# An MoE layer's last experts: down products by rows, then a spread to the tokens by a product with their weights; four last pairs instead of three; more gather buffers

## The chip, the cores and the metric

The kernel runs on 1 core of one Trainium2 chip. The metric is device time in microseconds (us) of one execution. The engines are named as in the profile: PE is TensorE's matrix product and PEld its weight load, DVE is VectorE, ACT is ScalarE, POOL is GpSimd, SP is SyncE, which here only issues transfers. A name with a q (ACTq, SPq) stands for transfers issued from that engine's queue.

## The reference

One layer for 256 tokens of width 512: cross attention over 4096 context tokens and the tokens themselves, then a state space block, then a mixture of experts. Only the last part is touched:

```python
def _L0_ffn_ref(hidden_states, gate_w, wg, wu, wd, sg, su, sd):
    # 256 tokens, HID 512, 32 experts of inner width 192, the best 6 per token
    scores = jax.nn.sigmoid(x @ gate_w)
    topk_w, topk_i = jax.lax.top_k(scores, TOP_K)
    topk_w = topk_w / (jnp.sum(topk_w, axis=-1, keepdims=True) + 1e-20)
    combine = jnp.sum(jax.nn.one_hot(topk_i, N_EXP, dtype=topk_w.dtype) * topk_w[..., None], axis=1)
    g = jnp.einsum('td,edf->tef', x, wg)
    u = jnp.einsum('td,edf->tef', x, wu)
    act = jax.nn.silu(g) * u
    routed = jnp.einsum('tef,efd,te->td', act, wd, combine)
    shared = jax.nn.silu(hidden_states @ sg) * (hidden_states @ su) @ sd
    return routed + shared
```

Here `x` is the layer norm of the residual, and the result is added to the residual. All is float32.

## The kernel before, in words

Attention and the state space block fill about the first 800 us and are not touched. Then the router ranks the tokens of every expert, sorts the experts so that those with the fewest tokens come last, and scatters the tokens' rows into one table in HBM (`xg`), a block of rows for each expert.

**Rounds.** The 32 experts go in 16 pairs, one pair a round (line 1524 on). Pairs 0 to 8 are wide: each expert has a block of 128 rows (`gate_up`, L1430; `down`, L1460). Pairs 9 to 15 are halves: the two experts of a pair share one block, 64 rows each (`gate_up_halves`, L1383; `down_halves`, L1406), and their products with 64 columns of weights run side by side on TensorE. A round n issues, in program order: gate and up of pair n (`ps_egu`, L218 or L1389); the fetch of pair n+2's token rows (`fetch`, L1354, for most pairs an indirect transfer on POOL); the transposes of pair n+1's rows (`xgTp`, L1370, copied out by DVE); the down product of pair n-1; an expert weight load for a later pair (`load_pair`, on POOL); and the transposes of pair n's hidden rows (`hidTp`, L1402 or L1448, copied out by ACT, L1404 or L1450). DVE makes the hidden rows from ACT's `si` and `ps_egu` (L1393, L1396).

**Two ways from the hidden rows to the tokens.**

- Rows (pairs 0 to 12): the down product gives the expert's rows; ACT copies them from PSUM to `y_sb` (L1414, L1472) and writes them to a table `ye` in HBM (L1415, L1474). Later each token gathers its rows from `ye` by an indirect transfer on POOL (`gather`, L1316, one for each of the 6 choices and each of the 2 token tiles, into `yk`) and DVE adds them, times the token's weight, to the residual `x_sb` (`add`, L1327, L1330). A choice whose expert is not in `ye` reads a row of zeros (`ZROW`).
- Spread (the last three pairs, 13 to 15; `TAIL` is 6 experts): `spread_halves` (L1417) multiplies the hidden rows with a matrix `spread` of 128 rows by 256 tokens that holds each row's weight in its token's column, so that the hidden values stand by tokens; ACT and DVE copy them (L1427, L1428, `hidS`). `down_into` (L1452) then makes the down product for both token tiles, three products of 128x512 each, and sums all three pairs in two PSUM tiles `total`. The matrix `spread` is made in round 3 by `weights_back` (L1494 to L1517): masks on DVE (L1500 to L1514), transposes on TensorE (`spreadT`, L1516).

At the end `finish` (L1567) adds `total` to `x_sb` for each token tile, and `store` (L1570) writes it out.

**What sets the order.** A scheduler places the instructions of each engine; every engine takes its own in order. The PSUM pool for down results has three buffers, of which `total` holds two in the last rounds. The gathers of the first token tile are issued in round 13, after pair 12's rows; those of the second after the first's adds. Their buffers come from three rings: the rings of `y_sb` and `xg_sb` (four buffers each) and a ring of its own, `yp` (three). `tc.issue_after(done[n])` keeps adds behind DVE's last hidden result of round n. Lines that the prediction uses: L1330, L1389, L1402, L1411 and L1412 (down by rows of a half pair), L1415, L1424, L1428, L1457, L1516, L1567.

Of the kernel before, what the change touches and what calls it, by code (L numbers as in the profile page):

```python
# [11 lines left out]
FP = mybir.dt.float32  # L12
# [48 lines left out]
TAIL = 6  # L61
# [12 lines left out]
def perceiver_layer(ctx: ExitStack, tc: tile.TileContext, a: dict, out: bass.AP):  # L74
# [65 lines left out]
    def layer(ctx, bounded):  # L140
# [936 lines left out]
        def rows_of(t):  # L1077

            V.tensor_scalar(m["dst"][:, t], m["iota"][:, 0:NE], float(L), None, ALU.mult)
            V.tensor_tensor(m["dst"][:, t], m["dst"][:, t], m["rank"][:, t], ALU.add)  # L1080
            V.tensor_tensor(own, m["hot"][:, t], m["dst"][:, t].unsqueeze(1).to_broadcast([P, TOPK, NE]), ALU.mult)
            V.tensor_reduce(m["rowf"][:, t, :], own, AX.X, ALU.add)
            V.tensor_copy(row[:, t, :], m["rowf"][:, t, :])

        def result_rows():
# [7 lines left out]
            for t in range(NT):  # L1093
                V.tensor_tensor(own, m["hot"][:, t], dst[:, t].unsqueeze(1).to_broadcast([P, TOPK, NE]), ALU.mult)
                V.tensor_reduce(m["rowf"][:, t, :], own, AX.X, ALU.add)
# [220 lines left out]
        def gather(src, rows, t, *rings):  # L1316

            got = []
            for k in range(TOPK):
                pool, tag = rings[k % len(rings)]  # L1320
# [11 lines left out]
        class Rounds:  # L1332


            def __init__(self, ctx, weights):
# [9 lines left out]
                self.rows, self.xgT, self.hid, self.hidT, self.done = {}, {}, {}, {}, {}  # L1345
# [60 lines left out]
            def down_halves(self, n, to):  # L1406
# [5 lines left out]
                TE.matmul(ps, h[:, 1, :], wd[2], start=False, stop=True)  # L1412
                y = self.e4.tile([P, DM], FP, tag="y", name="y_sb")
# [3 lines left out]
            def spread_halves(self, n, by):  # L1417

                h = self.hid.pop(n)

                whole = [pool.tile([P, 2, L], FP, tag=tag, name=name) for pool, tag, name in
                         ((self.ps_t, "t", "hid_sp"), (self.ps_ye, "ye", "rest_sp"))]
                for i in range(2):
                    TE.matmul(whole[i][:, 0, :], h[self.half(i), 0:P], by[self.half(i)], start=True, stop=True)  # L1424
                TE.matmul(whole[1][:, 1, :], h[:, P:2 * P], by, start=True, stop=True)
                hs = self.hidT[n] = self.e2.tile([P, 3, L], FP, tag="hidS", name="hidS")
                S.copy(hs[:, 0, :], whole[0][:, 0, :])  # L1427
                self.done[n] = V.tensor_copy(hs[:, 1:3, :], whole[1]).ins  # L1428
# [23 lines left out]
            def down_into(self, n, total, first, last, tiles=range(NT)):  # L1452
                wd = self.down_weights(n)
                h = self.hidT[n]
                for t in tiles:
                    for j in range(3):
                        TE.matmul(total[t], h[:, j, t * P:(t + 1) * P], wd[j],  # L1457
                                  start=(first and j == 0), stop=(last and j == 2))

# [16 lines left out]
        with ExitStack() as rctx:  # L1476
            main = Rounds(rctx, weights)
            yp = rctx.enter_context(tc.tile_pool(name="yp", bufs=3))
# [41 lines left out]
            def spread_last(n):  # L1520
                main.spread_halves(n, spread[:, n - LAST, :])

            got, r_y, r_x, r_k = None, (main.e4, "y"), (main.e4, "xg"), (yp, "yk")
# [52 lines left out]
            with arms.Else():  # L1576
# [20 lines left out]
                for t in range(NT):  # L1597
                    add(gather(ye2, row2, t, (main.e4, "xg")), t)
# [55 lines left out]
```

## Time and profile before

| | |
|---|---|
| median of 6 runs | 992.71 us (990.6 to 993.81) |
| profiled execution, device time | 992.73 us |
| its span, first to last instruction | 990.9 us |
| granted TensorE clock, mean | 0.997 |
| rounds of the experts | about 844 to 982 us |
| last weights and rows off the queues | about 953 us |
| first and last gather issued | 959.42 and 974.69 us |
| last add begins | 978.54 us |
| finishes of the two token tiles begin | 979.87 and 982.38 us |

The page of the profile gives each engine's busy time, the span in 40 slices, the transfers, the chain of work that ended last, and the costliest groups of instructions by line. The timeline lists instructions in order of time: start, length, engine, line, operation, tiles as out<-in with their shape, and how many were merged (x). In brackets stands the engine's idle time just before, and what ended it. A float32 product of 128x512 is two records (x2). Ends of products are modelled and overlap the next one, so costs on TensorE are read from start to start. Times of the table are microseconds from the start of the span.

### The profile page before, as it was taken

The page shows a single profiled execution, that of the slowest core. Times are in us where ns is not written, and L with a number is a line of the kernel's source. Part 1 is how long each engine was busy: PE and PEld are TensorE (multiplying, and loading weights), DVE is VectorE, ACT ScalarE, POOL GpSimd, SP SyncE. Part 2 cuts the span into 40 slices and gives each one's busy share as a digit, 9 for nine tenths or more (in the row PEclk, how much of TensorE's full clock was granted, in tenths as well). Part 3 has the DMA queues.
Part 4 walks back from the last instruction along what each step waited for, and adds up shares of the span by engine and source line. Part 5 has one row for each costly group of instructions (what it writes and reads, how often), then busy time and mean ns, then how long its engine had stood idle before and what let it go on. Part 6 is the DMA issues. An engine that isn't in the chain of part 4 may idle for free.

```text
span 990.9 us, 8901 instructions
## 1 busy us (share of the span) xinstructions
PE 968.8 (98%) x2742; PEld 456.3 (46%) x2742; DVE 498.5 (50%) x999; ACT 386.2 (39%) x851; POOL 205.6 (21%) x212
## 2 busy tenths in 40 slices
PE   7999999999999999999999999999999999999996
PEld 3444444444444444444444444444465655555442
DVE  4456554454453544534545544468596756422134
ACT  3645444443443444434434434353262822122210
POOL 4443001101100200200200200000013325454523
PEclk9999999999999999999999999999999999999998
DMA  8734132222313304304204112140055553999963
GB/s 318 234 74 116 56 114 91 51 38 111 85 22 127 85 4 145 86 0 149 69 16 141 41 32 65 63 127 1 0 176 178 209 174 117 331 351 352 390 228 113
DMA packets 131580, 125.91 MB, mean 127 GB/s; under 512 B 80225, under 2 KB 99586, under 8 KB 126274
## 3 DMA queue, kind: packets, MB, share of 16 engines
q1 hardware_dynamic: 119216, 77.96, 26.2%
q0 software_dynamic: 7984, 41.16, 11.4%
q10 hardware_dynamic: 4322, 6.11, 1.7%
q8 instruction: 24, 0.39, 0.2%
q14 instruction: 34, 0.28, 0.1%
HBM read 89.02 MB, written 36.19 MB: 126 GB/s over the span
## 4 chain that ended last, share of the span: by engine, by line
PE 93%; DMA 1%; DVE 1%; ACT 1%; POOL 1%; issue 1%; another core or an unknown queue 1%; SPq 0%; POOLq 0%; DVEq 0%; ACTq 0%
PE scT L567 23%; PE oT L592 23%; PE ps_kv L364 17%; PE ps_egu L218 4%; PE ps_self L218 3%; PE ps_v L218 2%; PE ps_o L790 2%; PE ps_ye L1466 2%; PE ps_xbc L218 1%; PE ps_out L984 1%; PE ps_egu L1389 1%; PE ps_k L218 1%; PE ps_sgu L218 1%; PE total L1457 1%; PE xgTp L1370 1%; PE ps_ye L1469 1%
## 5 line engine op out<-in xcount | busy, mean ns | idle before, releaser
L583 DVE TENSOR_TENSOR lacc<-lacc,prT 128x512 f32<-128x512 f32 x256 | 182.9, 715 | 239.0 <-ACT prT L573 238.3
L573 ACT ACTIVATE prT<-scT,bq,rk 128x512 f32<-128x512 f32 x256 | 198.8, 777 | 254.0 <-PE scT L567 241.8
L567 PE MATMUL scT<-qT,kT 128*128 128x512 f32 x536 | 271.6, 593 | 0.0
L592 PE MATMUL oT<-prT,v 128*128 128x512 f32 x528 | 268.3, 592 | 0.0
L567 PEld LDWEIGHTS scT<-qT,kT 128*128 128x128 f32 x536 | 101.1, 190 | 124.9 <-issue 122.2
L592 PEld LDWEIGHTS oT<-prT,v 128*128 128x128 f32 x528 | 100.2, 190 | 125.8 <-issue 115.8
L196 POOL TENSOR_TENSOR rk<-pv,mhalf 128x4 f32<-128x4 f32 x32 | 32.3, 1011 | 369.3 <-DVE pv L195 369.3
L364 PE MATMUL ps_kv<-wkv,fast 128*128 128x512 f32 x112 | 53.4, 592 | 0.0
L254 ACT ACTIVATE sq<-kraw 128x128 f32<-128x128 f32 x128 | 35.6, 278 | 45.2 <-DVE kraw L382 43.1
L364 PE MATMUL ps_kv<-wkv,ctx 128*128 128x512 f32 x112 | 52.8, 592 | 0.0
L364 PE MATMUL ps_kv<-fast,fast 128*128 128x512 f32 x112 | 52.6, 592 | 0.0
L598 DVE TENSOR_TENSOR oacc<-oT,oacc 128x512 f32<-128x512 f32 x64 | 43.7, 683 | 0.0
L364 PEld LDWEIGHTS ps_kv<-wkv,fast 128*128 128x128 f32 x112 | 21.3, 190 | 26.8 <-issue 26.8
L364 PEld LDWEIGHTS ps_kv<-fast,fast 128*128 128x128 f32 x112 | 21.3, 190 | 26.8 <-issue 21.8
L364 PEld LDWEIGHTS ps_kv<-wkv,ctx 128*128 128x128 f32 x112 | 21.3, 190 | 26.8 <-issue 23.7
L358 POOL TENSOR_TENSOR fast<-ctx 128x512 f32<-128x512 f32 x7 | 9.3, 1331 | 113.1 <-PE ps_kv L364 94.2
L382 DVE TENSOR_TENSOR kraw<-ps_kv,fast 128x256 f32<-128x256 f32 x42 | 17.8, 424 | 28.2 <-PE ps_kv L364 28.2
L1441 DVE TENSOR_TENSOR hid<-si,ps_egu 128x128 f32<-128x128 f32 x18 | 5.2, 288 | 53.1 <-ACT si L1439 42.9
L790 PE MATMUL ps_o<-wo,qT 128*128 128x512 f32 x64 | 28.8, 592 | 0.0
L218 PE MATMUL ps_self<-wq,xT 128*128 128x512 f32 x64 | 28.1, 592 | 0.0
L603 DVE RECIPROCAL lacc<-ps_l 128x512 f32<-128x512 f32 x8 | 26.8, 3348 | 0.1
L364 PE MATMUL ps_kv<-fast,ctx 128*128 128x512 f32 x56 | 26.3, 592 | 0.0
(392 smaller groups left out, 1129.9 us busy)
## 6 DMA issues: line engine op xcount, KB each, us to landing
xg<-xn SPq DMA_DIRECT2D x6, 2560.0 KB
ctx<-in_ctxT_dram SPq DMA_DIRECT2D x7, 1024.0 KB
kd<-tr SPq DMA_DIRECT2D x112, 64.0 KB
kT<-kd SPq DMA_DIRECT2D x28, 256.0 KB
ye<-y_sb ACTq DMA_DIRECT2D x22, 256.0 KB
wq<-in_wq_dram SPq DMA_DIRECT2D x4, 1024.0 KB
wo<-in_wo_dram SPq DMA_DIRECT2D x4, 1024.0 KB
w_in<-in_W_inT_dram SPq DMA_DIRECT2D x4, 1024.0 KB
```

The costliest lines, as they stand in the source:

```text
L196: return G.tensor_tensor(dst, v[:, :n], mhalf[:, :n], ALU.pow)
L218: TE.matmul(ps, lhs(k), rhs_of(k), start=(k == 0), stop=(k == KD - 1))
L254: S.activation(sq[:, h, :], raw[:, h, :], AF.Square, accum_out=ss[:, h:h + 1])
L364: TE.matmul(ps, lhs(k), rhs(k), start=(start and k == 0), stop=(k == 1), skip_group_check=True)
L567: scored.append(TE.matmul(sc, kT[:, g, i * P:(i + 1) * P], qT[:, t, heads4(g), :].rearrange("p h q -> p (h q)"), start=True, stop=True).ins)
L573: S.activation(pr, sc, AF.Exp, bias=shift, scale=SCALE if r is None else r[:, i, g:g + 1])
L583: V.tensor_tensor(la, la, pr, ALU.add)
L592: TE.matmul(outs[g, t], v[:, i, g * HD:(g + 1) * HD], pr, start=(n == 0), stop=last)
L598: V.tensor_tensor(ov, outs.pop((g, t)), ov, ALU.add)
L603: V.reciprocal(rl, ps)
L790: TE.matmul(m["ps_o", t], aT[:, t, h, :], wo[j][:, h % 4, :], start=(h == 0), stop=(h == NH - 1))
L1466: TE.matmul(ps[i], h[:, i, :], wd[i], start=True, stop=False)
```

## The change

1. `TAIL` is 8 instead of 6: the last four pairs (12 to 15) are spread, three before. `spread`, the masks and the row of zeros grow or move with it; `result_rows` and `rows_of` use the first 6 of the now 8 rows of a work tile.
2. For the last pairs the order is turned round. The hidden rows are transposed (`turn_hidden_halves`), the down product is made by rows (`down_rows`, now shared with `down_halves`) and copied to SBUF by ACT (`down_here`). Then one product for each token tile, with `spread` as the stationary operand and these rows as the moving one, sums into `total` (`spread`). In round n the down of pair n-1 and the spread of pair n-2 are issued.
3. The ring `yp` has six buffers instead of three, and the gathers no longer use the ring of `y_sb`. The gathers of both token tiles are issued one round earlier (rounds 12 and 13), without waiting for adds in program order; the row fetch of pair 15 is moved ahead of them. Three adds are kept behind round 14's hidden result, nine behind round 15's.

```diff
-TAIL = 6
+TAIL = 8
...
-            def spread_halves(self, n, by):
...
-                whole = [pool.tile([P, 2, L], FP, tag=tag, name=name) for pool, tag, name in
-                         ((self.ps_t, "t", "hid_sp"), (self.ps_ye, "ye", "rest_sp"))]
-                for i in range(2):
-                    TE.matmul(whole[i][:, 0, :], h[self.half(i), 0:P], by[self.half(i)], start=True, stop=True)
-                TE.matmul(whole[1][:, 1, :], h[:, P:2 * P], by, start=True, stop=True)
-                hs = self.hidT[n] = self.e2.tile([P, 3, L], FP, tag="hidS", name="hidS")
-                S.copy(hs[:, 0, :], whole[0][:, 0, :])
-                self.done[n] = V.tensor_copy(hs[:, 1:3, :], whole[1]).ins
+            def down_here(self, n):
+
+                self.y[n] = self.e4.tile([P, DM], FP, tag="y", name="y_sb")
+                S.copy(self.y[n], self.down_rows(n))
+
+            def spread(self, n, by, total, first, last, tiles=range(NT)):
+
+                for t in tiles:
+                    TE.matmul(total[t], by[:, t * P:(t + 1) * P], self.y[n], start=first, stop=last)
...
-            def down_into(self, n, total, first, last, tiles=range(NT)):
-                wd = self.down_weights(n)
-                h = self.hidT[n]
-                for t in tiles:
-                    for j in range(3):
-                        TE.matmul(total[t], h[:, j, t * P:(t + 1) * P], wd[j],
-                                  start=(first and j == 0), stop=(last and j == 2))
...
-            yp = rctx.enter_context(tc.tile_pool(name="yp", bufs=3))
+            yp = rctx.enter_context(tc.tile_pool(name="yp", bufs=6))
...
             for n in range(NP):
                 wide = 2 * n < WIDE
                 (main.gate_up if wide else main.gate_up_halves)(n)
-                if n == LAST + 1:
-                    add(got, 0)
-                    got = gather(ye, row_y, 1, r_y, r_x, r_y, r_x, r_x, r_k)
-                if FIRST <= n + 2 < NP:
-                    main.fetch(n + 2)
+
+                for f in range(n + 2, n + 4 if n == LAST else n + 3):
+                    if FIRST <= f < NP and f not in fetched:
+                        main.fetch(f)
+                        fetched.add(f)
...
                 elif n > LAST:
-                    if n == LAST + 1:
-                        total = [main.ps_ye.tile([P, DM], FP, tag="ye", name="total") for _ in range(NT)]
-                    if n == NP - 1:
-
-                        main.down_into(n - 1, total, False, False, [0])
-                        with tc.issue_after(main.done[n]):
-                            add(got, 1, range(0, TOPK // 2))
-                        spread_last(n)
-                        with tc.issue_after(main.done[n]):
-                            add(got, 1, range(TOPK // 2, TOPK))
-                        main.down_into(n - 1, total, False, False, [1])
-                    else:
-                        main.down_into(n - 1, total, n - 1 == LAST, False)
+                    main.down_here(n - 1)
+                if n == LAST:
+                    got.append(gather(ye, row_y, 0, r_k * TOPK))
+                elif n == LAST + 1:
+                    total = [main.ps_ye.tile([P, DM], FP, tag="ye", name="total") for _ in range(NT)]
+                    got.append(gather(ye, row_y, 1, r_x * 2 + r_k * 4))
+                if n > LAST + 1:
+                    spread_last(n - 2)
+                if n == NP - 2:
+                    add_behind(n, 0, 3)
+                if n == NP - 1:
+                    add_behind(n, 3, 2 * TOPK)
...
-                if n == LAST:
-                    got = gather(ye, row_y, 0, r_k, r_y, r_k, r_x, r_k, r_y)
-                if n < LAST:
-                    (main.turn_hidden if wide else main.turn_hidden_halves)(n)
-                elif n < NP - 1:
-                    spread_last(n)
-            main.down_into(NP - 1, total, False, True)
+                (main.turn_hidden if wide else main.turn_hidden_halves)(n)
+
+            spread_last(NP - 2, [0])
+            main.down_here(NP - 1)
+            spread_last(NP - 2, [1])
+            spread_last(NP - 1)
```

More of the change, by code (lines that the diff above doesn't have):

```diff
@@ L1080, in rows_of @@
             V.tensor_tensor(m["dst"][:, t], m["dst"][:, t], m["rank"][:, t], ALU.add)
-            V.tensor_tensor(own, m["hot"][:, t], m["dst"][:, t].unsqueeze(1).to_broadcast([P, TOPK, NE]), ALU.mult)
-            V.tensor_reduce(m["rowf"][:, t, :], own, AX.X, ALU.add)
+            V.tensor_tensor(own[:, 0:TOPK], m["hot"][:, t], m["dst"][:, t].unsqueeze(1).to_broadcast([P, TOPK, NE]), ALU.mult)
+            V.tensor_reduce(m["rowf"][:, t, :], own[:, 0:TOPK], AX.X, ALU.add)
             V.tensor_copy(row[:, t, :], m["rowf"][:, t, :])
@@ L1093, in result_rows @@
             for t in range(NT):
-                V.tensor_tensor(own, m["hot"][:, t], dst[:, t].unsqueeze(1).to_broadcast([P, TOPK, NE]), ALU.mult)
-                V.tensor_reduce(m["rowf"][:, t, :], own, AX.X, ALU.add)
+                V.tensor_tensor(own[:, 0:TOPK], m["hot"][:, t], dst[:, t].unsqueeze(1).to_broadcast([P, TOPK, NE]), ALU.mult)
+                V.tensor_reduce(m["rowf"][:, t, :], own[:, 0:TOPK], AX.X, ALU.add)
             V.tensor_scalar(m["m8"][:, :, 0:TOPK], m["rowf"], float(ZROW), None, ALU.min)
@@ L1308, in layer, with gather @@
         actx.close()
-        def gather(src, rows, t, *rings):
+        def gather(src, rows, t, rings):
             got = []
-            for k in range(TOPK):
-                pool, tag = rings[k % len(rings)]
+            for k, (pool, tag) in enumerate(rings):
                 yk = pool.tile([P, DM], FP, tag=tag, name="yk")
@@ L1344, in __init__ @@
                     G.memset(z, 0.0)
-                self.rows, self.xgT, self.hid, self.hidT, self.done = {}, {}, {}, {}, {}
+                self.rows, self.xgT, self.hid, self.hidT, self.y, self.done = {}, {}, {}, {}, {}, {}
             def row0(self, n):
@@ L1404, in turn_hidden_halves, with down_rows @@
                 S.copy(self.hidT[n], tp)
-            def down_halves(self, n, to):
+            def down_rows(self, n):
                 wd = self.down_weights(n)
@@ L1412, in down_halves @@
                 TE.matmul(ps, h[:, 1, :], wd[2], start=False, stop=True)
+                return ps
+            def down_halves(self, n, to):
+                ps = self.down_rows(n)
                 y = self.e4.tile([P, DM], FP, tag="y", name="y_sb")
@@ L1415, in down_halves @@
                 nc.scalar.dma_start(to[self.row0(n):self.row0(n) + P, :], y)
-            def spread_halves(self, n, by):
-                h = self.hid.pop(n)
-                whole = [pool.tile([P, 2, L], FP, tag=tag, name=name) for pool, tag, name in
-                         ((self.ps_t, "t", "hid_sp"), (self.ps_ye, "ye", "rest_sp"))]
-                for i in range(2):
-                    TE.matmul(whole[i][:, 0, :], h[self.half(i), 0:P], by[self.half(i)], start=True, stop=True)
-                TE.matmul(whole[1][:, 1, :], h[:, P:2 * P], by, start=True, stop=True)
-                hs = self.hidT[n] = self.e2.tile([P, 3, L], FP, tag="hidS", name="hidS")
-                S.copy(hs[:, 0, :], whole[0][:, 0, :])
-                self.done[n] = V.tensor_copy(hs[:, 1:3, :], whole[1]).ins
+            def down_here(self, n):
[4 more added lines that the diff above has]
+                    TE.matmul(total[t], by[:, t * P:(t + 1) * P], self.y[n], start=first, stop=last)
             def gate_up(self, n):
@@ L1519, in layer, with spread_last, add_behind @@
             FIRST, LAST = HEAD // 2, NP - TAIL // 2
-            def spread_last(n):
-                main.spread_halves(n, spread[:, n - LAST, :])
-            got, r_y, r_x, r_k = None, (main.e4, "y"), (main.e4, "xg"), (yp, "yk")
+            def spread_last(n, tiles=range(NT)):
+                main.spread(n, spread[:, n - LAST, :], total, n == LAST, n == NP - 1, tiles)
+            fetched = set()
+            got, r_x, r_k = [], [(main.e4, "xg")], [(yp, "yk")]
+            def add_behind(n, k0, k1):
+                with tc.issue_after(main.done[n]):
+                    for k in range(k0, k1):
+                        add(got[k // TOPK], k // TOPK, [k % TOPK])
             for n in range(NP):
@@ L1597, in layer @@
                 for t in range(NT):
-                    add(gather(ye2, row2, t, (main.e4, "xg")), t)
+                    add(gather(ye2, row2, t, [(main.e4, "xg")] * TOPK), t)
                     store(t)
```

## The prediction

> **What bounds the kernel now.** I read the page's busy table and slices first, then its chain of waits, then the stretch that the diff touches (the last three of the 16 rounds) in the timeline, TensorE alone first, then all engines. A round is one pair of experts; its start is the first gate-up product (L1389).
>
> ```profile
> PE 968.8 (98%) x2742; PEld 456.3 (46%) x2742; DVE 498.5 (50%) x999; ACT 386.2 (39%) x851; POOL 205.6 (21%) x212
> PE   7999999999999999999999999999999999999996
> PE 93%; DMA 1%; DVE 1%; ACT 1%; POOL 1%; issue 1%; another core or an unknown queue 1%; SPq 0%; POOLq 0%; DVEq 0%; ACTq 0%
> ```
>
> TensorE is busy in every slice, and 93% of the chain is its own products. So a change pays by what it takes out of TensorE's sequence, as long as nothing else becomes the last to finish. The rounds:
>
> ```profile
> 944.72 2.80 PE L1389 MATMUL ps_egu<-w_in,xgT 128*64 128x384 f32 x16
> 948.03 0.64 PE L1411 MATMUL ps_ye<-oacc,hidT 128*64 128x512 f32 x1
> 950.01 0.38 PE L1402 MATMUL hidTp<-ident,hid 128*128 128x128 f32 x2
> 950.32 0.54 PE L1389 MATMUL ps_egu<-lacc,xgT 128*64 128x384 f32 x1
> 956.96 0.54 PE L1389 MATMUL ps_egu<-w_in,xgT 128*64 128x384 f32 x1
> 966.69 0.54 PE L1389 MATMUL ps_egu<-wkv,xgT 128*64 128x384 f32 x1
> 969.42 1.12 PE L1457 MATMUL total<-w_in,hidS 128*128 128x512 f32 x2
> 971.37 1.12 PE L1457 MATMUL total<-wkv,hidS 128*128 128x512 f32 x2 [0.82 <-DVE hidS L1428]
> 980.46 1.02 PE L1457 MATMUL total<-ctx,hidS 128*128 128x512 f32 x2
> 981.32 1.02 PE L1457 MATMUL total<-v,hidS 128*128 128x512 f32 x2
> ```
>
> Start times differ by what a step costs; the printed lengths overlap. One 128x512 product into `total` is 981.32 - 980.46 = 0.86. Round 12, which goes down by rows, takes 950.32 - 944.72 = 5.60; rounds 13 and 14 take 6.64 and 9.73; from round 15's start to the end of the last product it is 981.32 + 0.86 - 966.69 = 15.49, with a stall on VectorE's `hidS` copy inside. The other side of the end, the gathers and adds:
>
> ```profile
> 956.44 0.33 ACTq L1415 DMA_DIRECT2D ye<-y_sb  x1
> 959.42 0.94 POOL L1322 DMA_INDIRECT yk<-ye,row_y  x1 [15.30 <-DMA ye<-y_sb]
> 974.69 1.13 POOL L1322 DMA_INDIRECT yk<-ye,row_y  x1 [0.30 <-issue]
> 978.54 0.75 DVE L1330 SCALAR_TENSOR_TENSOR x_sb<-yk,lacc,x_sb 128x512 f32<-128x512 f32 x1 [0.67 <-DMA yk<-ye,row_y]
> 979.87 0.69 DVE L1567 TENSOR_TENSOR x_sb<-total,x_sb 128x512 f32<-128x512 f32 x1 [0.58 <-PE total L1457]
> 982.38 0.69 DVE L1567 TENSOR_TENSOR x_sb<-total,x_sb 128x512 f32<-128x512 f32 x1 [1.81 <-PE total L1457]
> ```
>
> The adds end at 979.29, and both finishes (L1567) wait for `total`. So TensorE ends the kernel, but the adds are only 0.58 ahead of the first finish: a shorter TensorE tail must not outrun them.
>
> **TensorE, round by round.** Pieces: gate-up of a half pair 969.42 - 966.69 = 2.73; down by rows 950.01 - 948.03 = 1.98; the two transposes of `hid` 950.32 - 950.01 = 0.31; a spread product has the shape of L1457, 0.86.
> - Round 13 becomes a copy of round 12: 5.60 instead of 6.64, -1.04.
> - Round 14 is round 12 plus two spreads: 5.60 + 1.72 = 7.32 instead of 9.73, -2.41.
> - Round 15 to the end: 2.73 + 1.98 + 2 x 0.86 + 0.31 + 0.86 + 1.98 + 3 x 0.86 = 12.16 instead of 15.49, -3.33. The 18 products into `total` and nine spreads of `hid` are gone; eight spreads, three downs and six transposes have come. The 0.82 stall goes with `hidS`; next late there is ACT, below.
>
> Sum -6.78. On the old time axis round 14 starts at 955.92, round 15 at 963.24, the last product ends at 975.40.
>
> **Earlier work.** `spreadT` has eight transposes instead of six; six take 0.81 in the chain, so +0.27, on the path. On VectorE, in the order of the changed kernel, ten mask writes (0.24 each, from the row of five in 1.20) stand between the first pair's two `hid` results, not five: the second result comes at 850.29 + 2.40 = 852.69 instead of 852.13. But TensorE's order there also moves one more gate-up product (0.66) ahead of the transpose that waits 1.07 now. These cancel to about 0; bounds -0.1 and +0.6. The member products grow from 192 to 256 columns (0.36 each, nine of them, perhaps 0.07 more each); VectorE idles 1.64 there, and without that cover they cost 0.6.
>
> **The new hand-offs.** The last pair now runs transposes, ACT copy, down, ACT copy, spread. `hidT`: the copy can start 0.20 after TensorE moves on (950.01 to 950.21 for `y_sb`), takes 0.38, plus 0.05 to wake TensorE: 0.63, under one spread of 0.86. `y_sb`: 0.20 + 0.58 + 0.05 = 0.83 under the other 0.86. The trace shows no such chain at the end of the kernel; bounds 0 (both covered) and 0.63 + 0.83 = 1.46 (no cover). The margins of 0.23 and 0.03 are thin, so I take +0.2.
>
> **Gathers and adds.** The last row write that the gathers wait for is pair 11's (issued at 950.82, one round earlier), not pair 12's. Write to first gather is 959.42 - 956.44 = 2.98 now, so the first starts at 953.80; fetching pair 15's rows stays ahead of it in POOL's queue as it was. No weight load is queued behind. The twelfth issue is 15.27 after the first, 969.07, its add 3.85 later (974.69 to 978.54), ending 973.67. VectorE: three adds stand after the copy of `xgT` (960.52) and before round 15's `hid`, done by 962.77; `hid` is wanted at 966.45. Nine adds follow from 967.11: 9 x 0.75 = 6.75, to 973.86. With the 0.58 seen between last add and finish: 974.44. `total` of the first token tile ends at 974.54 and its finish starts 0.27 later (979.60 to 979.87), 974.81. So TensorE still ends it, by 0.37. The two stores then start 0.8 apart, not 2.5; if the second queued behind the whole landing of the first (2.04 for a row write in the chain of waits), that would be +1.2; I take 0, for the 16 DMA engines are 0.13 busy after 982.4 (windows view). The extra buffers cost nothing: gathers eight to ten (counted from 0) wait for adds done by 963, and the last for one done by 967.9.
>
> When gathers and adds meet now, a gather's issue takes up to 1.29 on POOL instead of 0.94, so they lose at most 0.35 each; most gathers will run before the adds, so I add nothing. The Trainium skill, "SBUF — State Buffer", section "SBUF: two separate sides", says that VectorE with two SBUF inputs and GpSimd lock each other out of a shared port for whole instructions (the first named case only against a GpSimd operation that reads SBUF). That speaks against the change: by this rule the five gathers that would meet adds could lose a whole add of 0.75 each, 3.75 in all, and less the room of 0.37 the sum would be near -2.9 instead of -6.3.
>
> **Sum.** -6.78 + 0.27 + 0 + 0.2 = -6.3. The profiled execution took 992.73 (span 990.9, 1.83 around it); the median of six runs is 992.71, the same within 0.02. So 986.4.
>
> **Rivals.**
> 1. The adds end it (0.16). Now adds without idle cover stand up to 0.91 apart (971.90 to 972.81). Nine at 0.91: 967.11 + 8.19 + 0.58 = 975.88, 1.1 after 974.81, so 987.5; a gather held longer puts it up to 988.5. For it: 0.37 of room. Against it: the gathers start 5.6 earlier.
> 2. The ACT copies are exposed (0.10): the 1.46 instead of 0.2, 987.7. For it: margins of 0.03. Against it: ACT is busy 0.70 us in the last 15.7.
> 3. The time is given back (0.06). ACT twice stands without a visible cause before `si` at 845 to 852 (4.36 and 1.84, put down to "remote"). ACT now feeds TensorE in each of the last steps; such holds there would cost 6.2, so 992.6, no change. For it: the changed code places such holds anew. Against it: the last rounds show none.
> 4. Slower (0.04): late gathers block `hid`. VectorE takes the three adds before round 15's `hid` in order. If the first gather started with round 15 (963.24, 9.4 late) instead of 953.80, the twelfth add would end at 963.24 + 15.27 + 4.60 = 983.11, the first finish 983.69, the second 984.38 against 975.6: +8.8, 995.2. It decides from a first gather at 961.24: 982.38, the second finish now, less 15.27 + 4.60 + 0.58 + 0.69. Against it: even now they start at 959.42, behind a later write.
>
> The forecast itself has 0.64 (985.4 to 987.4). A measurement here can tell about 0.2%, 2 us, from no change: faster takes forecast and rivals 1 and 2, 0.90; same rival 3, 0.06; slower rival 4, 0.04. The range reaches down by the bound of -0.1, covered hand-offs and the runs' own spread (990.6 to 993.81), to 984.4, and up past rivals 1 and 2, to 989.2; rivals 3 and 4 are left out.
>
> **What would show it.** Round 13 at 5.6, 14 at 7.3, 15 to the last product at 12.2 to 12.5; eight products on the spread line and no `hidS`; the first gather near 954; the last add ending before the first finish, whose idle time ends on TensorE; waits of TensorE on ACT in the tail under 0.3 in sum. The prediction is wrong if the finishes wait for adds or gathers, if TensorE's tail shows an idle over 1 us, or if round 0 grows.

## The result, and the profile after

The changed kernel takes 989.67 us (median of 23 runs, 986.49 to 991.87), the kernel before in the same sessions 992.12 (46 runs, 990.47 to 994.96). The ratio is 0.9972, with a 95% interval of 0.9965 to 0.9978: 2.8 us less, where 6.3 were forecast. The direction was right and the size was not. The profiled run of the changed kernel took 986.24 (span 984.5), a little under the fastest of these 23; set against the one profiled run of before (992.73) it shows 6.5 less, about what was forecast, and 0.96 of that lies ahead of round 12 (943.76 against 944.72). So the first trace alone would have passed for a confirmation. The question is what the typical run has on top of it.

The changed kernel's page, busy line and chain of waits:

```profile
PE 963.0 (98%) x2730; PEld 453.6 (46%) x2730; DVE 497.6 (51%) x1000; ACT 388.0 (39%) x854; POOL 204.9 (21%) x212
...
PE 95%; ACT 1%; DVE 1%; POOL 1%; DMA 1%; issue 1%; another core or an unknown queue 0%; SPq 0%; DVEq 0%; ACTq 0%
```

Its timeline, the last three rounds (start, length, engine, line; the brackets hold idle time and releaser):

```profile
949.36 0.54 PE L1388 MATMUL ps_egu<-lacc,xgT 128*64 128x384 f32 x1
...
953.47 0.94 POOL L1321 DMA_INDIRECT yk<-ye,row_y  x1 [10.30 <-DVE hid L1395]
...
954.96 0.54 PE L1388 MATMUL ps_egu<-w_in,xgT 128*64 128x384 f32 x1
...
962.28 0.54 PE L1388 MATMUL ps_egu<-wkv,xgT 128*64 128x384 f32 x1
...
966.36 0.33 ACT L1390 ACTIVATE si<-ps_egu 128x192 f32<-128x192 f32 x1 [3.55 <-PE ps_ye L1410]
...
967.40 6.43 DVE L1329 SCALAR_TENSOR_TENSOR x_sb<-yk,lacc,x_sb 128x512 f32<-128x512 f32 x9
...
968.42 1.21 POOL L1321 DMA_INDIRECT yk<-ye,row_y  x1 [0.70 <-issue]
...
969.86 0.58 ACT L1423 COPY y_sb<-ps_ye 128x512 f32<-128x512 f32 x1 [3.17 <-issue]
...
970.50 1.12 PE L1428 MATMUL total<-y_sb,xc 128*128 128x512 f32 x2 [1.57 <-issue]
...
973.53 2.82 PE L1428 MATMUL total<-y_sb,xc 128*128 128x512 f32 x6
...
975.60 1.48 DVE L1565 TENSOR_TENSOR x_sb<-total,x_sb 128x512 f32<-128x512 f32 x2 [1.76 <-PE total L1428]
```

Rounds 13 and 14 take 5.60 and 7.32, as forecast. Round 15 to the last product takes 973.53 + 2.82 - 962.28 = 14.07 and not 12.16. Its gate-up ends 2.73 after its start, at 965.01, but its silu (L1390, the `si` from which VectorE makes pair 15's `hid`) starts at 966.36, 1.35 late; a usual silu starts 0.12 after the product. The copy of pair 14's rows at 969.86 is late too, and TensorE stands still for 1.57 before it can spread them. The words "issue" and a stale product as releaser say that the profile knows no cause.

A second profile of the same kernel (e1_again) is more typical; timeline:

```profile
968.59 0.33 ACT L1390 ACTIVATE si<-ps_egu 128x192 f32<-128x192 f32 x1 [3.88 <-remote]
...
969.63 6.43 DVE L1329 SCALAR_TENSOR_TENSOR x_sb<-yk,lacc,x_sb 128x512 f32<-128x512 f32 x9
...
970.65 1.21 POOL L1321 DMA_INDIRECT yk<-ye,row_y  x1 [4.12 <-DVE x_sb L1329]
...
976.09 1.29 DVE L1565 TENSOR_TENSOR x_sb<-total,x_sb 128x512 f32<-128x512 f32 x2
```

Here round 15 starts at 962.31, the silu is 3.55 late, `hid` of pair 15 and the nine adds behind it follow, and the twelfth gather waits 4.12 for the fourth add. TensorE ends at 975.56, 0.8 earlier than in the first profile, yet the span is 987.0, 2.5 longer. So TensorE does not end this execution.

**What ends it.** The chain of waits stops at the second finish in every profile. The view of the closing line goes on, with the sequencers' records (engine and q; count; least, median and largest ns; first and last start). The kernel before:

```profile
L1650 POOLq DRAIN  x3: 40/107/6593, 983.5 to 990.6; - x3
L1650 SPq DRAIN  x3: 7/7/7, 989.4 to 990.3; - x3
```

The changed kernel, second profile:

```profile
L1648 POOLq DRAIN  x3: 40/107/6594, 979.6 to 986.7; - x3
L1648 SPq DRAIN  x3: 7/7/41, 984.0 to 986.4; - x3
```

POOL closes with a drain of 6.59 us. In these two profiles the drain stands behind the landing of the last gather, a step of 1.77 on POOL's queue, a branch, and 3.0 to 3.4 without a record. SP closes after the stores. The span ends 0.82 to 0.92 after the later of the two in all 20 profiles of this study (table below); from the start of the last gather to the end of POOL's drain it is 14.7 to 15.7. In the kernel before POOL's drain ends at 990.08 and SP's last wait at 989.35: **two chains, 0.7 apart** (0.6 in a second profile, e9_before), and the prediction saw only the one that passes through TensorE. In the first profile of the changed kernel SP is the later one, by 0.33; in the second POOL, by 2.1.

### The profile page after: what moved, and what is told of

Its sections match the earlier page's. It is cut to its first block, busy times and chain, and to the rows that moved or that the text cites. A ratio compares the mean times of both kernels' runs of the same rounds, so it can differ in the third digit from the quotient of the medians.

```text
span 984.5 us, 8877 instructions
## 1 busy us (share of the span) xinstructions
PE 963.0 (98%) x2730; PEld 453.6 (46%) x2730; DVE 497.6 (51%) x1000; ACT 388.0 (39%) x854; POOL 204.9 (21%) x212
## 4 chain that ended last, share of the span: by engine, by line
PE 95%; ACT 1%; DVE 1%; POOL 1%; DMA 1%; issue 1%; another core or an unknown queue 0%; SPq 0%; DVEq 0%; ACTq 0%
PE scT L567 23%; PE oT L592 23%; PE ps_kv L364 17%; PE ps_egu L218 4%; PE ps_self L218 3%; PE ps_v L218 2%; PE ps_o L790 2%; PE ps_egu L1388 2%; PE ps_ye L1458 2%; PE ps_k L218 1%; PE ps_xbc L218 1%; PE ps_out L984 1%; PE ps_sgu L218 1%; PE xgTp L1369 1%; PE ps_ye L1461 1%; PE ps_ye L1411 1%
```

## The experiments

The columns: ratio to the kernel before on the same chip with its interval; how late round 15's silu starts (its start less round 15's first product less 2.73; 0.11 to 0.17 is on time); start of the last gather; end of POOL's drain; SP's last wait over; end of the span. The first profile of before and of the changed kernel stand ahead. Two kinds of chip show up: e5 to e8 ran on one where the kernel before takes 990.0 and no signal of TensorE is late anywhere; all others where it takes 992.1 to 992.7 and some are. The silu is one signal of several: copies behind later products can be late too.

| kernel | ratio | silu late | last gather | POOL | SP | span |
|---|---|---|---|---|---|---|
| before | 1 | 0.12 | 974.69 | 990.08 | 989.35 | 990.9 |
| changed | 0.9972 (0.9965-0.9978) | 1.35 | 968.42 | 983.28 | 983.61 | 984.5 |
| e1_again | 0.9972 (0.9962-0.9982) | 3.55 | 970.65 | 986.17 | 984.03 | 987.0 |
| e2_three | 1.0004 (0.9995-1.0012) | 0.12 | 975.23 | 990.89 | 987.30 | 991.7 |
| e3_slack | 0.9973 (0.9961-0.9986) | 5.66 | 973.05 | 988.17 | 987.73 | 989.0 |
| e4_vector | 0.9984 (0.9973-0.9994) | 3.80 | 971.42 | 986.14 | 986.57 | 987.5 |
| e5_seven | 0.9953 (0.9940-0.9966) | 0.16 | 967.51 | 982.71 | 980.68 | 983.6 |
| e6_plain | 0.9929 (0.9914-0.9944) | 0.16 | none | - | 980.88 | 981.8 |
| e7_shift | 1.0103 (1.0088-1.0118) | 0.17 | 981.93 | 996.94 | 996.36 | 997.8 |
| e8_before6 | 1.0005 (0.9996-1.0014) | 0.11 | 972.86 | 987.81 | 987.00 | 988.7 |
| e9_before | 1.0000 (0.9989-1.0011) | 0.12 | 974.25 | 989.13 | 988.57 | 990.0 |
| e10_after | 0.9971 (0.9960-0.9982) | 3.90 | 971.58 | 987.28 | 984.66 | 988.1 |
| e11_seven | 0.9955 (0.9939-0.9971) | 5.04 | 967.37 | 982.47 | 985.71 | 986.6 |
| e12_both | 0.9961 (0.9945-0.9977) | 6.90 | 967.56 | 982.51 | 987.09 | 988.0 |
| s1_shift30 | 0.9978 (0.9968-0.9989) | 3.93 | 971.22 | 986.79 | 984.65 | 987.6 |
| s2_shift60 | 0.9990 (0.9980-1.0001) | 4.50 | 973.35 | 989.04 | 987.28 | 989.9 |
| s3_plain | 0.9925 (0.9908-0.9941) | 0.16 | none | - | 981.22 | 982.1 |
| s4_two | 0.9979 (0.9967-0.9992) | 6.45 | 970.77 | 985.43 | 991.21 | 992.1 |
| p1_paced | 0.9960 (0.9947-0.9973) | 0.16 | 969.96 | 985.18 | 982.86 | 986.0 |
| p2_half | 0.9964 (0.9952-0.9977) | 2.24 | 970.92 | 985.86 | 988.47 | 989.4 |

**e1_again**: no edit.

> The changed kernel once more, as a yardstick and for a second profile of it. Theory A (the missing time is TensorE waiting in the last round for ACT's copies of y_sb and hidT, whose start is held): -2 to -4 us against the kernel before; rounds 13 and 14 again take 5.60 and 7.32, and the stretch from round 15's first product to the last product is 12.16 plus the idle time shown on the lines of the spread and down products; more than 1 us of idle there. Rival B (the missing time is lost before round 13, in the stage around the weights of the mask or in the first rounds, and the 1.57 us of idle in the first profile is an accident): the last round takes 12.2 to 12.6, and round 13 starts less than 0.5 us earlier than in the kernel before.

Measured -2.8 again, with the silu 3.55 late and POOL, not TensorE, at the end. Rounds 13 and 14 again take 5.60 and 7.32. Rival B falls: round 13 starts 0.93 earlier than in before, and the last round takes 13.26. Theory A has its number, but the end is not TensorE's.

**e2_three**: the new order with three pairs.

```diff
-TAIL = 8
+TAIL = 6
```

> Down by rows and spread as in the changed kernel, but three last pairs instead of four. TensorE's rounds by the terms of the prediction: 13 and 14 take 5.60 each, 15 takes 12.16, so TensorE would end 8.5 us before the old end; but the row write that the gathers wait for is pair 12's again, so they start near 959.4 on the old axis and their adds end near 979.3, as before. Theory A: the adds end it, first finish near 979.9 and the second 0.8 behind instead of 2.5, so -1.3 to -2 us against the kernel before whatever ACT does; the holds of ACT in round 15 do not matter. Rival B (loss before round 13): the adds end it too, and the same loss lies on top: 0 to +2 us. If it came out at or below the changed kernel (-3 us or more), the fourth pair would be worth nothing.

Measured no change, outside the range of theory A and inside that of rival B, but for a reason that neither had. This trace is the cleanest test of the sum for TensorE; timeline:

```profile
962.06 0.54 PE L1388 MATMUL ps_egu<-wkv,xgT 128*64 128x384 f32 x1
...
971.48 2.82 PE L1428 MATMUL total<-y_sb,xc 128*128 128x512 f32 x6
...
975.23 1.03 POOL L1321 DMA_INDIRECT yk<-ye,row_y  x1 [0.30 <-issue]
...
980.06 1.29 DVE L1565 TENSOR_TENSOR x_sb<-total,x_sb 128x512 f32<-128x512 f32 x2
```

The closing line of the same run:

```profile
L1648 POOLq DRAIN  x3: 40/107/6593, 984.3 to 991.4; - x3
L1648 SPq DRAIN  x3: 7/7/7, 987.3 to 991.1; - x3
```

Round 15 to the last product is 12.24, forecast 12.16, so the new hand-offs through ACT cost nothing when signals come on time. TensorE ends 8 us earlier than before and the kernel gains nothing: the last gather starts at 975.23 as ever (974.69 before), and POOL closes 3.6 behind SP. **The whole gain of the change hangs on the fourth pair, which lets the gathers start a round earlier.**

**e3_slack**: more of TensorE's work between each copy and its use.

```diff
-                if n > LAST + 1:
-                    spread_last(n - 2)
+                if n == NP - 1:
+                    spread_last(n - 3)
...
-            spread_last(NP - 2, [0])
+            spread_last(NP - 3)
             main.down_here(NP - 1)
-            spread_last(NP - 2, [1])
+            spread_last(NP - 2)
             spread_last(NP - 1)
```

> The changed kernel with the same products, but the spreads put one round later, so that between each ACT copy of the last pair and its use TensorE has two spreads (1.72 us) in place of one (0.86): pair 12 spreads in round 15 ahead of hidT(15), pair 13 behind it, pair 14 behind the last down. Theory A (ACT's copies are late in round 15): 1 to 3 us below the changed kernel, -4 to -6 against the kernel before; round 13 and 14 take 5.60, round 15 to the end about 13.9 to 14.3, sum near 25.1 as the products alone cost. Rival B: equal to the changed kernel within 0.5 us. Rival C (TensorE itself stands still in round 15, whoever copies): equal within 0.5 us, with an idle on TensorE that no copy explains.

Measured the same as the changed kernel: theory A in its plain form (thin margins between copy and use) fails. The silu itself is 5.66 late, and this order of the spreads does not hide that; timeline:

```profile
970.99 0.33 ACT L1390 ACTIVATE si<-ps_egu 128x192 f32<-128x192 f32 x1 [6.73 <-remote]
971.21 0.58 ACT L1423 COPY y_sb<-ps_ye 128x512 f32<-128x512 f32 x1
```

**e4_vector**: two of the copies on VectorE.

```diff
-                S.copy(self.hidT[n], tp)
+                (V.tensor_copy if n == NP - 1 else S.copy)(self.hidT[n], tp)
...
-                S.copy(self.y[n], self.down_rows(n))
+                (V.tensor_copy if n == NP - 2 else S.copy)(self.y[n], self.down_rows(n))
...
-                if n == NP - 1:
-                    add_behind(n, 3, 2 * TOPK)
...
+            add_behind(NP - 1, 3, 2 * TOPK)
             spread_last(NP - 2, [0])
```

> The changed kernel with two of the last copies taken off ACT: y_sb of pair 14 and hidT of pair 15 are copied by VectorE, two and three adds deep in its order. Theory A with ACT's own sequencer as the cause (its instructions come late): 1 to 2 us below the changed kernel. Theory A' (the signal of TensorE's product is what comes late, to whoever waits): VectorE starts its copies as late as ACT did, no gain, within 0.5 us of the changed kernel or up to 0.8 slower, because an add of 0.75 stands ahead of a copy. Rival B: within 0.5 us.

Measured 0.9984, against the changed kernel in the same session (e1_again) 0.8 us slower by the medians, with overlapping intervals. The time fits theory A', but alone it does not clear ACT: the silu, still on ACT, is 3.80 late here too, and VectorE's two copies stand behind the late `hid`. The semaphore records of e3_slack say more: the signals of the gate-up, down and spread products that end at 965.4 to 969.0 are recorded between 970.91 and 971.10, and the silu (970.99) and the copy behind it follow at once. The products run ahead; the news that they are done comes late, in a bunch. So TensorE's signals are late, and not ACT.

**e5_seven**: one gather buffer more, so that the twelfth gather waits for the third add, ahead of pair 15's `hid`, and not for the fourth, behind it.

```diff
-            yp = rctx.enter_context(tc.tile_pool(name="yp", bufs=6))
+            yp = rctx.enter_context(tc.tile_pool(name="yp", bufs=7))
```

> The changed kernel with seven gather buffers in place of six, so that the twelfth gather waits for the third add (before round 15's hid) and no longer for the fourth (behind it). Theory P (the end is set by POOL: from the landing of the last gather to the end of the span it is 12.5 us in every trace so far, 978.45 to 990.91 in the kernel before, 974.16 to 986.99 in the second profile of the changed one; the last gather is late because it waits behind hid(15)): the last gather is issued before 968.5 and lands before 972, POOL's chain ends near 984, and the time falls to -4.5 to -6 us against the kernel before, 2 to 3 below the changed kernel. Rival T (TensorE's tail sets the end, through the finishes and the stores): within 0.5 us of the changed kernel.

Measured -4.7 us: theory P (POOL's chain sets the end) holds, T (TensorE's tail does) falls. POOL still closes 2 us behind SP.

**e6_plain**: gathers replaced by plain transfers.

```diff
-                G.indirect_dma_start(out=yk, out_offset=None, in_=src,
-                                     in_offset=bass.IndirectOffsetOnAxis(ap=rows[:, t, k:k + 1], axis=0))
+                nc.sync.dma_start(yk, src[(t * TOPK + k) * P:(t * TOPK + k + 1) * P, :])
```

> The changed kernel with its twelve gathers replaced by plain transfers of fixed rows of ye on SP's queue: it leaves out which rows are added. Theory G (TensorE's signals reach ACT late in round 15 because POOL issues gathers one behind the other at that time): signals on time, silu of pair 15 starts within 0.2 us of the end of its gate-up product, the tail takes 12.2 to 12.5, -5.5 to -7.5 against the kernel before. Theory F (late signals come with the load of TensorE's own instructions): signals as late as in the changed kernel, 1.5 us or more in round 15; time -4 to -6, since POOL's end is early here too.

Measured -7.0, but this chip shows no late signal in any kernel, so it decides nothing between G (POOL's gathers make the signals late) and F (the loads of TensorE's own instructions do). It does bound the change: with the gathers off POOL, the new tail of TensorE is worth 7.

**e7_shift**: small products at the start.

```diff
+        d = ps_d.tile([P, 8], FP, name="d")
+        for _ in range(48):
+            TE.matmul(d, ident, ident[:, 0:8], start=True, stop=True)
```

> The changed kernel with 48 small products (128x8, never read) ahead of TensorE's first work, where it stands idle until 5.47; they shift by 96 instructions where its instruction loads fall (16 KB each, 256 instructions apart by the records), so the load seen at 962 to 966 should come 8 to 11 us earlier. Theory F: no signal later than 0.7 us in round 15, hid(15) near 966.5, the last gather lands before 972.5, -4.5 to -6.5 against the kernel before if the small products are hidden, and at most 3 us more if not. Theory G: round 15 as late as in the changed kernel, -2 to -3.

Ill made: a 128x8 product of two f32 passes took 0.43, 20.65 in all, and most of it showed (+10.2). It says one thing: with signals on time and six buffers, the twelfth gather starts 14.09 after the first (967.84), not 17 to 17.7 as in e1_again and e10_after.

**e8_before6**: the kernel before with gathers free of its adds.

```diff
-            yp = rctx.enter_context(tc.tile_pool(name="yp", bufs=3))
+            yp = rctx.enter_context(tc.tile_pool(name="yp", bufs=6))
...
-                    got = gather(ye, row_y, 1, r_y, r_x, r_y, r_x, r_x, r_k)
+                    got = gather(ye, row_y, 1, r_x, r_y, r_x, r_y, r_x, r_y)
...
-                got = gather(ye, row_y, 0, r_k, r_y, r_k, r_x, r_k, r_y)
+                got = gather(ye, row_y, 0, r_k)
```

> The kernel before with the buffers alone: six yk buffers and the second token tile in the free xg and y buffers, so that no gather waits for an add. Gathers then come every 1.25 us from 959.42 on, the last issue near 973.2 and not 974.69. Theory P: POOL ended the kernel before by 0.7 us (its last drain ends 990.08, SP's last wait is over at 989.41), so -0.4 to -0.9, and then SP's stores end it. Rival T: 0.0 within 0.2.

Measured no change, against what P was taken to expect. P is not at fault, the premise was: the twelfth gather starts 15.23 after the first, as in before (15.27). Its gathers were not waiting for buffers; beside adds each takes up to 1.36 instead of 0.94. Buffers alone bring nothing.

**e9_before, e10_after, e11_seven, e12_both**: four kernels on one chip; e12 has the edits of e3 and e5.

> The kernel before, unchanged, for a profile on the same chip as the three that follow. By all theories 0.0 within 0.2 us against itself. What it tells: whether TensorE's signals are late here near the first gate-up products of the rounds (2.1 to 2.4 us in every profile of the first chip, none in the four profiles of the second), and which chain ends the kernel: theory P expects POOL's last drain to end 0.5 to 1 us behind SP's last wait, and 12.2 to 12.8 us from the landing of the last gather to the end of the span.

> The changed kernel, unchanged, on the same chip. Theory P with late signals as a matter of the chip: with signals on time, hid(15) is ready near 966.5 on the first chip's axis, the twelfth gather is issued 1.5 us behind it, and the time is -4.3 to -6 against the kernel before; with late signals as on the first chip -2.3 to -3.2. Rival (the changed kernel is always 2 us worse than the same with seven buffers): -2.3 to -3.2 with signals on time too.

> Seven gather buffers, as run before on another chip (-4.7 there). Theory P: -4.3 to -5.5 here too, whether signals are late or not, because its twelfth gather waits for nothing in round 15; with signals on time within 0.5 us of the changed kernel, with late ones 1.5 to 2.5 below it.

> Seven gather buffers, and the spreads one round later as in the run that gave TensorE more work between a copy and its use. Theory P: POOL's chain ends it as with seven buffers, so within 0.4 us of that kernel. Rival T: up to 1.6 us below it where signals are late, for TensorE's waits on ACT go.

Measured 0, -2.9, -4.5 and -3.9. The chip shows late signals. In e11 the gathers are free (last at 967.37) and POOL is done at 982.47, but now SP ends it at 985.71: pair 15's `hid` is late, so are the adds behind it and the finishes. e12's more patient order does not help, for the adds wait for `hid`, not for spreads. Round 9 starts at 926.61 (before) and 926.70 (changed), so in this pair of profiles the earlier stages cost 0.1.

**s1_shift30, s2_shift60**: is it TensorE's own instruction loads? 30 or 60 small bf16 products at the start, hidden in its first idle time (0.96 and 1.76 us long).

```diff
+        zb = zp.tile([P, P], mybir.dt.bfloat16, name="zb")
+        G.memset(zb, 0.0)
+        d = ps_d.tile([P, 8], FP, name="d")
+        for _ in range(30):
+            TE.matmul(d, zb, zb[:, 0:8], start=True, stop=True)
```

> The changed kernel with 30 small bf16 products (128x8, never read) at the very start, where TensorE idles until 5.47: TensorE's instruction loads fall 60 instructions earlier, about one round. Theory F (a signal of TensorE is late about where its own instruction load falls): on a chip with late signals the load seen at 962 to 966 comes 5 to 7 us earlier and the late signals with it, into rounds 13 and 14, round 15's signals late by under 0.7 us; the last gather is issued before 969.5 on the old axis. Other theories: late by 1.5 us or more in round 15 as in the changed kernel. On a chip without late signals this run tells nothing of it.

> The same with 60 small products, 120 instructions, about two rounds. Theory F: the late signals now lie 10 to 13 us earlier, in rounds 12 and 13, round 15 on time. Other theories: as the changed kernel. Time: at most 3 us of the small products are not hidden; beyond that as the first gather and hid(15) have it.

The load starts between 962.0 and 966.1 in the changed kernel's two earlier profiles, in e10_after and in its variants e3 and e4; here it moved to 956.5 and 952.0. The late signals did not move: round 15's silu is 3.93 and 4.50 late. Theory F falls.

**s3_plain, s4_two**: the plain transfers on a chip with late signals; and the gathers with two adds only.

```diff
-                        add(got[k // TOPK], k // TOPK, [k % TOPK])
+                        if k % TOPK == 0: add(got[k // TOPK], k // TOPK, [0])
```

> The plain transfers in place of the gathers once more (it leaves out which rows are added), for a chip with late signals. Theory G (POOL's back-to-back gathers make the signals late): round 15 on time, the late ones near the first gate-up products of the rounds stay. Theory F: round 15 late by 1.5 us or more. The time against the kernel before: -7 to -7.5 under G (as on the chip without late signals), -4.5 to -6 under F.

> The changed kernel with two adds in place of twelve (it leaves out ten of the gathered rows). Theory D (VectorE's adds back to back beside the gathers make the signals late): round 15 on time. Theory F or G: late as in the changed kernel. POOL's chain: no gather waits for an add behind hid(15), so its end is as with seven buffers, -4.3 to -5.5 against the kernel before, unless late signals of TensorE then set the end through the finishes, -4 to -4.7.

Without gathers the silu is on time (s3, timeline):

```profile
966.26 0.33 ACT L1389 ACTIVATE si<-ps_egu 128x192 f32<-128x192 f32 x1 [2.36 <-PE ps_egu L1387]
```

while the first round's two silus, behind products that end near 846 and 849, are as late in this run as in the others of such chips (1.9 and 2.3). With two adds it is late by 6.45 (s4, timeline):

```profile
969.52 0.95 POOL L1321 DMA_INDIRECT yk<-ye,row_y  x1 [0.30 <-issue]
...
970.77 0.95 POOL L1321 DMA_INDIRECT yk<-ye,row_y  x1 [0.30 <-issue]
...
974.09 0.33 ACT L1390 ACTIVATE si<-ps_egu 128x192 f32<-128x192 f32 x1 [8.65 <-remote]
```

Theory D falls and G holds, on one profile each: it takes POOL's gathers. The time of s4 (0.9979, -2.1) misses what was expected: POOL is done at 985.43, but behind the late signals TensorE stands still for 3.46 and SP ends at 991.21. With hardly an add in their way all twelve gathers start 1.25 apart here. In the kernel before and in e2_three they meet adds from the fourth on and start 1.25 to 1.6 apart, and no silu of round 15 is late. That left the pace.

**p1_paced, p2_half**: seven buffers, and a pause on POOL ahead of most gathers (p1) or of every second one (p2: `k % 2`).

```diff
+                if src is ye and k:
+                    with tc.issue_after(issued):
+                        G.memset(yk[:, 0:P], 0.0)
-                G.indirect_dma_start(out=yk, out_offset=None, in_=src,
-                                     in_offset=bass.IndirectOffsetOnAxis(ap=rows[:, t, k:k + 1], axis=0))
+                issued = G.indirect_dma_start(out=yk, out_offset=None, in_=src,
+                                              in_offset=bass.IndirectOffsetOnAxis(ap=rows[:, t, k:k + 1], axis=0)).ins
```

> Seven gather buffers, and a POOL memset (128x128 of the coming buffer, about 0.2 us) ahead of each gather but the first of a tile, so that gathers start about 1.5 us apart, as they do in the kernel before where adds lengthen them, and not 1.25. Theory G' (TensorE's signals are late behind a long run of gathers 1.25 us apart; the products near 846 stand behind such a run of twelve too, in every kernel): on a chip with late signals round 15 on time within 0.7 us, those near 846 late as ever; the last gather 2 to 2.5 us later than without pauses, so POOL ends it: -4 to -5.5 against the kernel before, within 0.7 of the kernel with seven buffers. Rival (it is the number of gathers, not their pace): round 15 late by 3 us or more as with seven buffers, and -3 to -4.5.

> The same with a pause ahead of every second gather, so 1.25 and 1.5 us apart in turn. Theory G': late by less than the 4.9 us seen with seven buffers and no pauses, 0 to 2.5; last gather 1 to 1.3 us later; -4.5 to -6 against the kernel before. Rival: late by 3 us or more, -3.5 to -4.7.

p1, timeline:

```profile
961.97 0.54 PE L1391 MATMUL ps_egu<-wkv,xgT 128*64 128x384 f32 x1
...
964.86 0.33 ACT L1393 ACTIVATE si<-ps_egu 128x192 f32<-128x192 f32 x1 [2.36 <-PE ps_egu L1391]
...
969.96 0.95 POOL L1324 DMA_INDIRECT yk<-ye,row_y  x1 [0.27 <-POOL yk L1323]
...
974.23 1.29 DVE L1568 TENSOR_TENSOR x_sb<-total,x_sb 128x512 f32<-128x512 f32 x2
```

The pauses came out smaller than meant. In p1 the gathers start 1.49 apart on average, 1.42 for the eight that have begun when the silu is due; the silu is on time (964.86, gate-up over at 964.70) and the tail takes 12.23, with the same twelve gathers and adds. In p2 they start 1.33 apart on average, and the silu is 2.24 late, as theory G' had it; a copy behind it is late as well, TensorE stands still for 3.21, and the time (-3.6) is in the rival's range. The other traces point the same way. With eight gathers begun when the silu is due, before and e9_before (1.37 apart) and p1 (1.42) are on time, while e3_slack (1.28) and e12_both (1.30) are 5.66 and 6.90 late. So it looks as if the pace decides, but by one profile for each kernel, on different chips, and with less than 0.1 between on time and late. And p1's own profile is mild elsewhere: of the first round's two silus, where nothing was paced, one is on time and one 1.9 late, against 1.7 to 3.1 for both in all other profiles of such chips. What p1 wins on TensorE it pays on POOL, whose last gather is 2.6 later than in e11: 0.9960 against 0.9955, no difference. The best complete kernel of the study is the changed one with seven buffers: -4.5 to -4.7 against the kernel before, 1.75 below the changed kernel by the medians of one session.

## Why the prediction was wrong, point by point

- **TensorE's rounds (-6.78): right.** 5.60, 7.32, and 12.24 where signals are on time (e2_three), 12.23 (p1_paced). e6_plain and s3_plain, where POOL's gathers are gone, gain 7.0 and 7.4. One wait was overlooked: in five runs (e5, e6, s3, s4, p2) round 13 takes 5.86 to 6.60, for TensorE waits there, up to 0.93, for the landing of pair 14's rows.
- **Earlier work (+0.27 and 0): right or a little dear.** Eight transposes show 1.02 against 0.81, and round 3, which holds them, takes 10.16 against 9.95. On the chip without late signals rounds 0 to 2 take 24.58 in the kernel before (e8_before6) and 24.51 in the changed order (e5_seven).
- **Hand-offs (+0.2, bounds 0 to 1.46): right as a price, about 0.** Rival 2 is out.
- **"So TensorE still ends it, by 0.37": the step that failed.** The end was read from the chain of waits, which stops at the last finish, and everything behind it was taken as a constant. In truth POOL's chain, from the last gather to the end of its drain, already ended the kernel before, by 0.7, and e2_three shows the price of missing that: 8 us off TensorE, no gain.
- **"The twelfth issue is 15.27 after the first, 969.07 ... and the last for one done by 967.9": the size that failed.** From 969.07 POOL's chain would end about 15.2 later, at 984.3, a time of 987 and close to the forecast. But the last gather starts at 970.65 and 971.58 in the two later profiles, since the fourth add stands behind pair 15's `hid`, and that is 3.5 to 3.9 late; POOL's drain then ends at 986.17 and 987.28, and these executions take 988.8 and 989.9, around the measured 989.67. The wait was listed and priced as never late. Without it (e11_seven) 1.75 of the missing 3.5 come back; the rest is then lost on the other path, where the late `hid` holds the adds and finishes and SP ends the kernel. Where no signal is late (e5_seven), POOL's chain alone keeps the gain at 4.7.
- **Rival 3 (0.06): right in its mechanism, wrong in path and chance.** The holds of unknown cause did return in the tail, 1.35 to 3.9 us in the changed kernel. They reach the end through the adds, the twelfth gather and POOL, not through TensorE. In the trace of before such holds (the two silus of the first round, 2.3 and 1.9 late) stood behind a run of twelve indirect transfers on POOL, 834.8 to 849.3; asking what POOL did there would have raised the chance.
- **Rival 1 (adds):** half right: in e1_again the first finish follows the last add without idle time, but the adds were late because `hid` was, not because gathers slowed them. **Rival 4** did not occur; gathers start at 952.95 to 954.60, forecast 953.80.
- **The shared port.** In the first profile nine adds take 6.43, with no wait; two gathers beside three adds took 1.45 and 1.27 instead of 0.95. So a meeting cost a gather up to 0.5, over the 0.35 taken, under the 0.75 by the rule of the Trainium skill, "SBUF — State Buffer", section "SBUF: two separate sides". That its sum (-2.9) is near the result is a coincidence: the time went elsewhere.

Still open: why the signals are late at all (by what path a run of gathers holds up TensorE's signals), and why one chip shows none at such a pace (e5_seven, 1.30 apart on average when the silu is due, on time). The pace and the number of gathers under way at once were not told apart. How the changed kernel itself does on that chip was not tried. One more difference between the chips is on record: in every profile of the chips with late signals, after 800 us, the trace holds 24 to 40 signal records of TensorE fewer than TensorE has signals (some 885), 27 to 38 fewer of VectorE and 20 to 26 fewer of ACT; on the other chip none is lacking. A lacking record is not a late signal: in p1_paced some are lacking and the copies that wait for these signals are on time.

## What to carry to other kernels

Before you price a shorter critical engine, list every chain that has to finish for the kernel to end, with the sequencers' closing records, and see by how much the second is behind; here it was 0.7 us, and ahead. A wait that is "never late" because its producer is early deserves a second look when that producer stands behind work whose holds you can't explain; one more buffer took it away and gained 1.75 us. And compare several profiles before believing one that agrees.

## What the runs showed of the hardware

- POOL's closing drain takes 6.59 us in every profile with gathers at the end; from the last gather's start to the end of that drain it is 14.7 to 15.7.
- A run of gathers 1.25 to 1.35 us apart on average goes with late completion signals of TensorE, by 1.35 to 6.9 us with eight to ten gathers begun, on all chips but one; at 1.37 to 1.42 they are on time in three profiles. The Trainium skill, "Perfetto Trace Analysis", section "Tensor Engine Instruction (MATMUL, LD_WEIGHTS)", says that the end of a TensorE instruction in a profile is estimated, and that its semaphore follows only when the write is acknowledged. This case shows the two apart: 0.02 where signals are on time (e5_seven, a down product that ends at 964.70 and its signal at 964.72), and 5.5 in e3_slack (965.40 and 970.91). Whether the acknowledgement is what is late, no run here shows.
- The clock can fall after such a wait. In e3_slack TensorE stood idle for 2.66 before 971.69, and the stretches view (busy time of PE, PEld, DVE, ACT, POOL; then the granted clock, DMA share, GB/s) reads:

```profile
970.00:972.00 2.00, 0.31 (x1) 0.14 (x1) 0.64 (x3) 0.81 (x2) 0.00 (x0) 1.00 0.33 113
972.00:974.00 2.00, 1.97 (x6) 0.77 (x5) 1.97 (x3) 0.37 (x1) 0.95 (x1) 0.80 0.00 0
974.00:976.00 2.00, 2.00 (x6) 0.30 (x4) 2.00 (x4) 0.00 (x0) 0.26 (x1) 0.50 0.47 127
```

The clock is halved for 3.4 us from 973.20, 1.5 after the wait. The same comes behind idle times of 3.21 (p2_half), 3.46 (s4_two, 6.8 us of half clock) and 3.9 (e12_both); behind 1.57 (the changed kernel), 1.84 (e4_vector) and 2.04 (e11_seven) the clock stays full up to the last product. So a late signal can cost more than its own length.
